# Graph attention on one core: products of a quarter and their sums in separate steps

## The chip, the cores and the metric

The kernel runs on one core of a Trainium2 chip. The core has five engines that are used here: TensorE (PE; its weight loads are listed as PEld), VectorE (DVE), ScalarE (ACT), GpSimd (POOL) and SyncE (SP), each with its own queue of instructions in a fixed order. An instruction waits at the head of its queue until what it needs is there, and everything behind it waits too. The metric is the device time of one execution in microseconds (us); shown is the median of three.

## The reference

A small graph network on 12500 nodes of 128 features and 200000 edges: a two-layer graph convolution with a layer norm, then an attention over the edges, with a second layer norm. The part that matters here is the attention, with `row` the source and `col` the destination of an edge:

```python
scores = einsum('ehd,ehd->eh', q[row], k[col]) / sqrt(16) + edge_emb @ eb_w.T + eb_b
seg_max = segment_max(scores, row)
exp_scores = exp(scores - seg_max[row])
attn = exp_scores / (segment_sum(exp_scores, row)[row] + 1e-10)
out = segment_sum(attn[..., None] * v[col], row)
```

There are 8 heads of 16 features.

## The kernel before

The kernel sorts the edges first, then does the two rounds of the convolution (spread and sum), the node layers between them, and then the attention; a last node stage writes the output. The change touches the attention alone, the function `attention`.

The edges are sorted by source node and cut into tiles of 128 edges, so that all edges of a tile belong to one block of 128 nodes. Four tiles (`G`) are a quarter, four quarters (`QN`) a group of 2048 edges; there are 104 groups, 416 quarters, 1664 tiles. The loop at the end of `attention` runs over steps `s`, one new quarter a step; in a step each stage works on an older quarter, and how much older is set by the constants `EXPAND, SCORE, WEIGH, ADD`.

- `take` (step s): POOL gathers the k and v rows of four tiles from DRAM into `kvg`, by indirect DMA, with 11 buffers (`KVB`), one for each quarter in flight.
- `turn` (every second step): VectorE builds `oht`, the one-hot matrices that pick an edge's source node, for two quarters.
- `expand` (quarter s - 2): TensorE makes q[row] of four tiles, `qe`, by `oht` times the block of `q_all`; the number of the block is fetched into a register of TensorE's queue first (line 889).
- `score` (quarter s - 3): VectorE multiplies `qe` with the gathered k and sums over each head into `sc`.
- `maxima`: once per group, a chain in seven pieces over TensorE, VectorE and ScalarE that finds the running maximum of each node. `sc` is completed (L1281) and turned (`st`, L1283), scanned both ways (`fw`, `bw`), the ends turned (`ro`, L1291 and L1292), copied by ScalarE (L1295, L1296), scanned along the tiles (`lu`, L1303 and L1305), turned back (`near`, `cp`, `cs`), combined (`mxs`, `dt`), turned (`wt`, `mr`, L1329 and L1331); ScalarE writes the exponentials into `kvg`, and a last pair (`dl`, L1339) gives the factor `fall` by which older sums shrink. The loop lets the chain go on by one piece at each `yield` of the other two generators. So its first piece comes at the end of the step in which the group's last quarter was scored, and all others in the next step, here called the chain step.
- `mark` (quarter s - 9): ScalarE builds `oh`, the one-hot matrix for the sum.
- `weigh` (quarter s - 9): VectorE multiplies v by the exponentials (L1358).
- `add_up` (quarter s - 10): for each of four tiles TensorE makes the product `ps` of `oh` and the weighted rows (L1379, 136 columns: 128 sums and 8 denominators), and VectorE adds it to the node block in `acc1` (L1381, the last of a quarter L1384), whose block number it fetches into a register. `ps` has three PSUM buffers of one bank each; the addition of a tile is issued after the product and the fetch of the next one. With a group's first quarter, the old sums are first scaled by `rs` (L1371, L1373, L1376).

PSUM has eight banks: two for `qe`, three for the buffers with the tag "g", which the chain's tiles `st`, `ro`, `cp`, `wt`, `mr` and also `rs` share, and three for `ps`.

The order of instructions in each queue is the order in which the program issues them; no planner moves them. In a step TensorE's queue holds `qe` of one quarter and `ps` of another, with pieces of the chain between and before them. VectorE's holds weigh, multiply, reduce, then the additions, with pieces of the chain between them. (`weigh` is called before the generators run.)

Of the kernel before, what the change touches and what calls it, by code (L numbers as in the profile page):

```python
# [9 lines left out]
F32 = mybir.dt.float32  # L10
# [6 lines left out]
P = 128  # L17
H = 8
HD = 16
W = P + H  # L20
G = 4
# [58 lines left out]
def kernel(  # L80
# [21 lines left out]
    nc = tc.nc  # L102
# [41 lines left out]
    ident = const.tile([P, P], F32, name="ident")  # L144
# [1056 lines left out]
    def attention(wp, psp):  # L1201
# [4 lines left out]
        T = TPP  # L1206
        QN = T // G
        kvs, scs, ohts, seqs, recs, mks, gts, ohs, fall = ({} for _ in range(9))
        a17 = wp.tile([1, H, T + 1], F32, name="a17")
# [66 lines left out]
        def maxima(g):  # L1276
# [4 lines left out]
            nc.vector.tensor_add(sc, sc, recs.pop(g)[:, :, :H].rearrange("p t h -> p h t"))  # L1281
            st = psp.tile([P, P], F32, tag="g", name="st", bufs=3)
            nc.tensor.transpose(st, sc.rearrange("p h t -> p (h t)"), ident)  # L1283
# [5 lines left out]
                                         op0=ALU.add, op1=ALU.max)  # L1289
            ro = psp.tile([1, 2, P], F32, tag="g", name="ro", bufs=3)  # L1290
            nc.tensor.transpose(ro[:, 0, :], fw[:, P - 1:], ident)  # L1291
# [20 lines left out]
            for k in range(2):  # L1312
                nc.vector.tensor_tensor(
                    near[:, k], luv[:, k, :, k:k + T],
                    gc[:, k * T:(k + 1) * T].unsqueeze(1).to_broadcast([1, H, T]), op=ALU.add)
            cp = psp.tile([P, 2], F32, tag="g", name="cp", bufs=3)
            for k in range(2):
# [9 lines left out]
            nc.vector.tensor_tensor(dt, st, mxs, op=ALU.subtract)  # L1327
            wt = psp.tile([P, H, T], F32, tag="g", name="wt", bufs=3)
            nc.tensor.transpose(wt.rearrange("p h t -> p (h t)"), dt, ident)  # L1329
            mr = psp.tile([1, H, T], F32, tag="g", name="mr", bufs=3)  # L1330
            nc.tensor.transpose(mr.rearrange(flat), mxs[:, :1], ident)  # L1331
            for q in range(QN):
# [22 lines left out]
        def weigh(i):  # L1355
# [3 lines left out]
                                 .to_broadcast([P, G, H, HD]))  # L1359

        def add_up(i):

            g, q = divmod(i, QN)
            t = kvs.pop(i)
            o = ohs.pop(i)
            for k in range(G):
                b = block_no(blk_si, i * G + k, [DVE])
                a = acc1[:, ds(b, 1), :].rearrange("p o w -> p (o w)")
                if q == 0 and k == 0:
                    rs = psp.tile([P, H], F32, tag="g", name="rs", bufs=3)  # L1370
                    nc.tensor.matmul(rs, o[0:1, 0, :], fall.pop(g), start=True, stop=True)  # L1371
                    av = a[:, :P].rearrange("p (h d) -> p h d", h=H)
                    nc.vector.scalar_tensor_tensor(  # L1373
                        av, rs.unsqueeze(2).to_broadcast([P, H, HD]), 1.0, av,
                        op0=ALU.add, op1=ALU.mult)
                    nc.vector.scalar_tensor_tensor(a[:, P:], rs, 1.0, a[:, P:],  # L1376
                                                   op0=ALU.add, op1=ALU.mult)
                ps = psp.tile([P, W], F32, name="ps", bufs=3)
                nc.tensor.matmul(ps, o[:, k, :], t[:, k, P:], start=True, stop=True)  # L1379
                if k:  # L1380
                    nc.vector.tensor_add(*adds)  # L1381
                    yield
                adds = a, a, ps
            nc.vector.tensor_add(*adds)  # L1384
            yield


        EXPAND, SCORE, WEIGH, ADD = 2, 3, 9, 10
        NQ = NG * QN
# [4 lines left out]
        for s in range(NQ + ADD):  # L1394
# [12 lines left out]
            if 0 <= s - EXPAND < NQ:  # L1407
                expand(s - EXPAND)
            i = s - SCORE
            bulk = []  # L1410
# [107 lines left out]
```

## Time and profile before

| what | value |
|---|---|
| median of three runs | 10037.43 us (10016.77 to 10048.95) |
| the profiled execution's own time | 8137.72 us |
| its span, first to last instruction | 8135.9 us |
| attention, first gather to last addition | about 5527 to 7980 us |
| busy in the span: PE, DVE, POOL, ACT | 71%, 70%, 55%, 26% |
| mean granted TensorE clock | 0.813 (about 0.72 in the attention) |
| a group of the attention, mean over 103 | 23.35 us |

The profile is of one execution, and that one was some 1900 us shorter than the median of the plain runs. Durations below are from it. A timeline row gives start, duration, engine, line, operation, output and inputs, and in brackets the idle time of the engine before it with what ended it. "Issue" is idle time in which the engine waited for nothing that the profile shows, such as a register fetch. The granted clock of TensorE is 1 at full and 0.5 at half speed; matrix instructions of f32 come in pairs (two passes), so four `ps` products are 8 instructions.

### The profile page before, as it was taken

What the parts mean: (1) busy time and instruction counts of PE and PEld (TensorE: products, weight loads), DVE (VectorE), ACT (ScalarE), POOL (GpSimd) and SP (SyncE); (2) the same over time, 40 slices, a digit from 0 to 9 for tenths busy, and PEclk for the clock granted to TensorE, in tenths of its full rate; (3) what the DMA queues carried; (4) which work ended last, traced back from release to release, by engine and by line L of the source; (5) the groups of instructions that cost most, each with busy time, mean ns of one, the idle gap of its engine ahead of it and who ended that gap; (6) DMA issues with size and microseconds to landing.
All of it is one profiled execution on the core that took longest, in us unless ns stands there. A gap on an engine that the chain in (4) does not pass through costs nothing.

```text
span 8135.9 us, 117573 instructions
## 1 busy us (share of the span) xinstructions
PE 5811.8 (71%) x32059; PEld 4415.2 (54%) x32059; DVE 5697.5 (70%) x11412; ACT 2087.4 (26%) x5494; POOL 4507.0 (55%) x4450
## 2 busy tenths in 40 slices
PE   5777781222899988859993788536777777777775
PEld 2344440121677777747772777535655566666564
DVE  8988785986555688765552666676777777777778
ACT  1222220001344300014441000013444444444442
POOL 0000005872777677777777777506666666666660
PEclk9999895555999999979996999867777777777775
DMA  3333233001577677736663666634444444444463
GB/s 84 94 90 94 84 106 90 6 5 29 157 197 197 198 209 204 195 48 194 196 195 78 193 192 193 147 114 140 123 123 124 120 124 123 124 119 123 124 114 71
DMA packets 570541, 1045.40 MB, mean 128 GB/s; under 512 B 131594, under 2 KB 294678, under 8 KB 557252
## 3 DMA queue, kind: packets, MB, share of 16 engines
q0 software_dynamic: 220992, 514.28, 26.6%
q1 hardware_dynamic: 348928, 523.60, 19.7%
q8 instruction: 297, 4.87, 0.2%
q14 instruction: 324, 2.65, 0.1%
HBM read 722.51 MB, written 314.96 MB: 128 GB/s over the span
## 4 chain that ended last, share of the span: by engine, by line
PE 32%; DVE 31%; DMA 12%; issue 10%; POOL 10%; DVEq 3%; ACT 2%; SPq 1%; POOLq 0%; ACTq 0%
PE ex L1016 13%; DMA got<-msg,idx_b 9%; DVE count_oh L234 6%; DVE key_d L460 4%; PE bc L1002 4%; POOL got L809 4%; POOL placed L809 4%; PE qe L1259 3%; DVE acc L1381 3%; POOL kvg L809 2%; DVE key_s L460 2%; PE ps L1379 2%; DVE kvg L1358 2%; PE bp L764 2%; DVE kvg L1269 2%
## 5 line engine op out<-in xcount | busy, mean ns | idle before, releaser
L809 POOL DMA_INDIRECT kvg<-kv,rec_in x1664 | 1634.1, 982 | 1073.1 <-issue 430.1
L809 POOL DMA_INDIRECT placed<-rec,idx_s x1664 | 1729.1, 1039 | 588.1 <-issue 503.0
L1055 PE MATMUL ps<-got,oh 128*128 128x128 f32 x8704 | 1214.0, 290 | 420.4 <-DMA got<-msg,idx_b 238.5
L1055 PEld LDWEIGHTS ps<-got,oh 128*128 128x128 f32 x8704 | 1073.2, 196 | 561.1 <-DVE acc L1061 261.6
L809 POOL DMA_INDIRECT got<-msg,idx_b x1088 | 1116.9, 1027 | 382.4 <-issue 130.7
L1007 DVE TENSOR_SCALAR oht<-bc,iota_col 128x512 f32<-128x512 f32 x976 | 732.3, 751 | 696.4 <-PE bc L1002 695.8
L1016 PE MATMUL ex<-h_all,oht 128*128 x7808 | 1134.7, 289 | 0.0
L1016 PEld LDWEIGHTS ex<-h_all,oht 128*128 128x128 f32 x7808 | 949.1, 192 | 222.3 <-issue 220.5
L1379 PE MATMUL ps<-kvg,oh 128*128 128x136 f32 x3328 | 785.8, 378 | 241.4 <-DVE acc L1381 240.8
L1259 PE MATMUL qe<-q_all,oht 128*128 x3328 | 902.7, 409 | 53.0 <-DVE oht L1248 11.2
L1259 PEld LDWEIGHTS qe<-q_all,oht 128*128 128x128 f32 x3328 | 685.9, 257 | 270.1 <-issue 189.2
L1379 PEld LDWEIGHTS ps<-kvg,oh 128*128 128x128 f32 x3328 | 635.6, 263 | 324.3 <-DVE acc L1381 308.7
L1020 ACT COPY et<-ex 128x512 f32<-128x512 f32 x976 | 571.3, 585 | 819.2 <-PE ex L1016 367.4
L1047 DVE TENSOR_TENSOR oh<-loc_b,iota_row 128x512 f32<-128x512 f32 x1088 | 753.8, 693 | 18.8
L1381 DVE TENSOR_TENSOR acc<-acc,ps 128x136 f32 x1248 | 365.7, 293 | 445.8 <-PE ps L1379 234.7
L949 POOL IOTA iota_t<- 128x1664 f32 x1 | 1.5, 1528 | 1165.2 <-PE pair_ps L239 1165.2
L1061 DVE TENSOR_TENSOR acc<-acc,ps 128x128 f32 x1088 | 308.7, 284 | 411.3 <-PE ps L1055 407.8
L1351 ACT ACTIVATE sq<-iota_row,loc_s 128x128 f32<-128x128 f32 x1664 | 529.8, 388 | 10.1
L751 ACT COPY attr_t<-tp 128x512 f32<-128x512 f32 x391 | 228.7, 585 | 955.8 <-PE tp L749 955.8
L764 PE MATMUL bp<-attr_t,ebw_at 128*64 128x512 f32 x782 | 444.2, 651 | 1.6 <-DVE attr_t L753 1.6
L1002 PE MATMUL bc<-seq_l,ones_bf 1*128 1x512 bf16 x976 | 377.1, 387 | 56.8 <-DMA seq_l<-seq_a 56.8
L460 DVE TENSOR_TENSOR key_s<-key_s 128x512 f32<-128x512 f32 (+1 forms) x468 | 397.6, 903 | 25.9 <-ACT key_s L475 23.1
(361 smaller groups left out, 6818.3 us busy)
## 6 DMA issues: line engine op xcount, KB each, us to landing
msg<-et SPq DMA_DIRECT2D x488, 258.0 KB
msg<-et SPq DMA_DIRECT2D x488, 256.0 KB
attr<-in_edge_attr_dram SPq DMA_DIRECT2D x97, 896.0 KB
seq_in<-row_seq SPq DMA_DIRECT2D x104, 512.0 KB
placed<-rec,idx_s POOLq DMA_INDIRECT x1664
kvg<-kv,rec_in POOLq DMA_INDIRECT x1664
got<-msg,idx_b POOLq DMA_INDIRECT x1088
masks<-mk SPq DMA_DIRECT2D x16, 832.0 KB
```

Source lines behind the costliest of these rows:

```text
L460: nc.vector.tensor_tensor(to, lo, hi, op=op)
L764: nc.tensor.matmul(sums[i // RQ][:RQ * H].rearrange("h g p -> h (g p)"), ebw_at[:, (RQ - 1 - r) * H:(2 * RQ - 1 - r) * H], tts.pop(i).rear ...
L809: nc.gpsimd.indirect_dma_start(out=out_, out_offset=None, in_=table, in_offset=bass.IndirectOffsetOnAxis(ap=idx, axis=0))
L1002: nc.tensor.matmul(bcs[t], ones_bf[:1, :], seqs[t // SQ][:, t % SQ * SA:][:, :SA], start=True, stop=True)
L1007: nc.vector.tensor_scalar(ohs[t].rearrange("p k c -> p (k c)"), bcs.pop(t), iota_col, None, op0=ALU.is_equal)
L1016: nc.tensor.matmul(exs[t][:, k, :], o[:, k, :], hb, start=True, stop=True)
L1020: nc.scalar.copy(ets[t][:, :, :D], exs.pop(t))
L1047: nc.vector.tensor_tensor(oh[t], loc_b[:, t, :].unsqueeze(2).to_broadcast([P, R, P]), iota_row.unsqueeze(1).to_broadcast([P, R, P]), op=AL ...
L1055: nc.tensor.matmul(ps[t], o[:, k, :], x_[:, k, :D], start=(k == 0), stop=(k == R - 1))
L1259: nc.tensor.matmul(qe[:, k, :], o[:, c * P:(c + 1) * P], qb, start=True, stop=True)
L1379: nc.tensor.matmul(ps, o[:, k, :], t[:, k, P:], start=True, stop=True)
L1381: nc.vector.tensor_add(*adds)
```

## The change

- `add_up` is split. A new `total` issues all four products of a quarter on TensorE, into two PSUM tiles of two products each (280 columns: two of 136 and 8 for `rs`). `add_up` does only the additions, a step later, each right after the fetch of its block number.
- `ps` has four buffers of one bank. The chain's `st` and `wt` share one bank (`sw`), and `ro`, `cp` and `mr` another (`sm`), with a single buffer each; `rs` lies in the first tile of `ps`.
- The constants go from `EXPAND, SCORE, WEIGH, ADD = 2, 3, 9, 10` to `EXPAND, SCORE, WEIGH, TOTAL, ADD = 1, 2, 8, 9, 10`: everything between the gather and the products comes one step earlier, the additions stay where they were. The gather's 11 buffers are freed by `total`.
- In the loop `total` is called after `expand`, before the generators. So in TensorE's queue the four products follow `qe` at once, and all pieces of the chain that belong to the step come after them: `ro` before stood ahead of the products and now stands behind them, and `cp` before stood ahead of the fourth product.
- With the lags, a group's chain step is now at step 4g + 6 (before 4g + 7). `turn` runs at even steps, before at a step ahead of and after the chain step, now in it; the scaling with `rs` before came in the step ahead of the chain step and is now in it.

```diff
--- before.py
+++ after.py
@@ -1205,7 +1205,7 @@
 
         T = TPP
         QN = T // G
-        kvs, scs, ohts, seqs, recs, mks, gts, ohs, fall = ({} for _ in range(9))
+        kvs, scs, ohts, seqs, recs, mks, gts, ohs, fall, sums = ({} for _ in range(10))
         a17 = wp.tile([1, H, T + 1], F32, name="a17")
         f17 = wp.tile([1, H, T + 1], F32, name="f17")
         loc_s = wp.tile([P, NT], F32, name="loc_s")
@@ -1279,7 +1279,8 @@
             mk = mks.pop(g)
             gl, gc = gts.pop(g)
             nc.vector.tensor_add(sc, sc, recs.pop(g)[:, :, :H].rearrange("p t h -> p h t"))
-            st = psp.tile([P, P], F32, tag="g", name="st", bufs=3)
+            sw = psp.tile([P, 2, P], F32, name="sw", bufs=1)
+            st, wt = sw[:, 0, :], sw[:, 1, :].rearrange("p (h t) -> p h t", h=H)
             nc.tensor.transpose(st, sc.rearrange("p h t -> p (h t)"), ident)
             yield
             fw = wp.tile([P, P], F32, name="fw", bufs=1)
@@ -1287,7 +1288,9 @@
             bw = wp.tile([P, P], F32, name="bw", bufs=1)
             nc.vector.tensor_tensor_scan(bw[:, ::-1], mk[:, 1, ::-1], st[:, ::-1], NEG,
                                          op0=ALU.add, op1=ALU.max)
-            ro = psp.tile([1, 2, P], F32, tag="g", name="ro", bufs=3)
+            sm = psp.tile([P, 4 * P], F32, name="sm", bufs=1)
+            ro = sm[:1, :2 * P].rearrange("o (k c) -> o k c", k=2)
+            mr, cp = sm[:1, 2 * P:3 * P], sm[:, 3 * P:3 * P + 2]
             nc.tensor.transpose(ro[:, 0, :], fw[:, P - 1:], ident)
             nc.tensor.transpose(ro[:, 1, :], bw[:, :1], ident)
             was = wp.tile([1, H], F32, name="was", bufs=2)
@@ -1313,7 +1316,6 @@
                 nc.vector.tensor_tensor(
                     near[:, k], luv[:, k, :, k:k + T],
                     gc[:, k * T:(k + 1) * T].unsqueeze(1).to_broadcast([1, H, T]), op=ALU.add)
-            cp = psp.tile([P, 2], F32, tag="g", name="cp", bufs=3)
             for k in range(2):
                 nc.tensor.matmul(cp[:, k:k + 1], near[:, k].rearrange(flat), one,
                                  start=True, stop=True)
@@ -1325,10 +1327,9 @@
                                                op0=ALU.add, op1=ALU.max)
             dt = wp.tile([P, P], F32, name="dt", bufs=1)
             nc.vector.tensor_tensor(dt, st, mxs, op=ALU.subtract)
-            wt = psp.tile([P, H, T], F32, tag="g", name="wt", bufs=3)
             nc.tensor.transpose(wt.rearrange("p h t -> p (h t)"), dt, ident)
-            mr = psp.tile([1, H, T], F32, tag="g", name="mr", bufs=3)
-            nc.tensor.transpose(mr.rearrange(flat), mxs[:, :1], ident)
+            nc.tensor.transpose(mr, mxs[:, :1], ident)
+            mr = mr.rearrange("o (h t) -> o h t", h=H)
             for q in range(QN):
                 nc.scalar.activation(
                     kvs[g * QN + q][:, :, 2 * P:],
@@ -1358,34 +1359,40 @@
             nc.vector.tensor_mul(v, v, kvs[i][:, :, 2 * P:].unsqueeze(3)
                                  .to_broadcast([P, G, H, HD]))
 
+        def total(i):
+
+            g, q = divmod(i, QN)
+            t, o = kvs.pop(i), ohs.pop(i)
+            two = []
+            for k in range(G):
+                if k % 2 == 0:
+                    two.append(psp.tile([P, 2 * W + H], F32, name="ps", bufs=4))
+                if q == 0 and k == 0:
+                    nc.tensor.matmul(two[0][:, 2 * W:], o[0:1, 0, :], fall.pop(g),
+                                     start=True, stop=True)
+                nc.tensor.matmul(two[-1][:, k % 2 * W:][:, :W], o[:, k, :], t[:, k, P:],
+                                 start=True, stop=True)
+            sums[i] = two
+
         def add_up(i):
 
-            g, q = divmod(i, QN)
-            t = kvs.pop(i)
-            o = ohs.pop(i)
+            two = sums.pop(i)
             for k in range(G):
                 b = block_no(blk_si, i * G + k, [DVE])
                 a = acc1[:, ds(b, 1), :].rearrange("p o w -> p (o w)")
-                if q == 0 and k == 0:
-                    rs = psp.tile([P, H], F32, tag="g", name="rs", bufs=3)
-                    nc.tensor.matmul(rs, o[0:1, 0, :], fall.pop(g), start=True, stop=True)
+                if i % QN == 0 and k == 0:
+                    rs = two[0][:, 2 * W:]
                     av = a[:, :P].rearrange("p (h d) -> p h d", h=H)
                     nc.vector.scalar_tensor_tensor(
                         av, rs.unsqueeze(2).to_broadcast([P, H, HD]), 1.0, av,
                         op0=ALU.add, op1=ALU.mult)
                     nc.vector.scalar_tensor_tensor(a[:, P:], rs, 1.0, a[:, P:],
                                                    op0=ALU.add, op1=ALU.mult)
-                ps = psp.tile([P, W], F32, name="ps", bufs=3)
-                nc.tensor.matmul(ps, o[:, k, :], t[:, k, P:], start=True, stop=True)
-                if k:
-                    nc.vector.tensor_add(*adds)
-                    yield
-                adds = a, a, ps
-            nc.vector.tensor_add(*adds)
-            yield
-
-
-        EXPAND, SCORE, WEIGH, ADD = 2, 3, 9, 10
+                nc.vector.tensor_add(a, a, two[k // 2][:, k % 2 * W:][:, :W])
+                yield
+
+
+        EXPAND, SCORE, WEIGH, TOTAL, ADD = 1, 2, 8, 9, 10
         NQ = NG * QN
         for g in range(3):
             load_records(g)
@@ -1406,6 +1413,8 @@
                 turn(s // 2)
             if 0 <= s - EXPAND < NQ:
                 expand(s - EXPAND)
+            if 0 <= s - TOTAL < NQ:
+                total(s - TOTAL)
             i = s - SCORE
             bulk = []
             if 0 <= i < NQ:
```

## The prediction

> **What bounds the kernel now.** I read the page's slices first: the attention stage is the last 30% of the span (about 5527 to 7980 us), where PE, DVE and POOL all stand near 7 tenths and none is full. So the limit is an order, not a load. Next came the stage's waits, then the timeline of one group of four quarters. A group is delimited by its one `sc` addition (L1281); 104 of them from 5551.1 to 7956.1 us make 23.35 us a group on average. The group below, 6578.15 to 6601.46, has 23.31. First its three stretches, in the table of busy time by window (length, busy us of each engine, granted TensorE clock):
>
> ```profile
> core 0: us, PE busy (x) PEld busy (x) DVE busy (x) ACT busy (x) POOL busy (x), PEclk, DMA share, GB/s
> 6578.15:6582.59 4.44, 3.97 (x16) 3.45 (x17) 3.23 (x10) 0.41 (x2) 3.25 (x4) 0.53 0.67 212
> 6582.59:6586.93 4.34, 3.07 (x11) 1.94 (x10) 2.83 (x12) 0.58 (x4) 1.59 (x2) 0.50 0.27 79
> 6586.93:6601.46 14.53, 11.03 (x50) 8.96 (x50) 11.18 (x27) 8.84 (x26) 10.69 (x11) 0.82 0.37 108
> ```
>
> The stretches are `sc` to `lu` (L1303), `lu` to `dl` (L1339), and `dl` to the next `sc`. Over all groups their means are 4.51, 4.17 and 14.67 us (medians 4.46, 4.34, 14.53). DVE is busy 17.2 us of 23.3; TensorE runs at half clock in the first two. VectorE's timeline of the round before (start, duration, idle time before it and who ended it):
>
> ```profile
> 6568.72 0.68 DVE L1358 TENSOR_TENSOR kvg<-kvg 128x512 f32<-128x512 f32 x1
> ...
> 6570.03 0.69 DVE L1271 TENSOR_REDUCE sc<-kvg 128x32 f32<-128x512 f32 x1
> 6570.97 0.30 DVE L1381 TENSOR_TENSOR acc<-acc,ps 128x136 f32 x1 [0.24 <-issue]
> 6571.58 0.29 DVE L1381 TENSOR_TENSOR acc<-acc,ps 128x136 f32 x1 [0.32 <-DVE acc L1381]
> ...
> 6572.60 0.30 DVE L1384 TENSOR_TENSOR acc<-acc,ps 128x136 f32 x1
> 6572.81 0.75 DVE L1248 TENSOR_SCALAR oht<-seq_in,iota_col 128x1024 f32<-128x1024 bf16 x1
> ...
> 6575.40 0.28 DVE L1373 SCALAR_TENSOR_TENSOR acc<-rs,acc 128x128 f32 x1
> 6575.71 0.17 DVE L1376 SCALAR_TENSOR_TENSOR acc<-rs,acc 128x8 f32 x1
> 6576.31 0.30 DVE L1381 TENSOR_TENSOR acc<-acc,ps 128x136 f32 x1 [0.43 <-DVE acc L1376]
> ...
> 6578.15 0.38 DVE L1281 TENSOR_TENSOR sc<-sc,rec_in 128x128 f32<-128x128 f32 x1
> ...
> 6582.37 0.29 DVE L1381 TENSOR_TENSOR acc<-acc,ps 128x136 f32 x1 [1.21 <-PE ps L1379]
> 6582.59 0.42 DVE L1303 TENSOR_TENSOR_SCAN lu<-gl_in,a 1x136 f32<-1x136 f32 x1
> ...
> 6586.93 0.15 DVE L1339 TENSOR_TENSOR dl<-was,mr 1x8 f32<-1x8 f32 x1 [0.64 <-PE mr L1331]
> ```
>
> An ordinary step lasts 4.09 us (6568.72 to 6572.81). Additions follow at 0.62 us though each takes 0.30: the block number is fetched into a register before each (0.30 us for the fetch, 0.09 for the address, on VectorE's own queue), and whether the products are there hardly matters. Only in the chain step does VectorE really wait for TensorE: 1.21 us before 6582.37. TensorE's timeline shows why:
>
> ```profile
> 6576.66 0.50 PE L1379 MATMUL ps<-kvg,oh 128*128 128x136 f32 x2 [1.57 <-DVE acc L1381]
> 6578.59 0.47 PE L1283 MATMUL st<-ident,sc 128*128 128x128 f32 x1 [1.43 <-DVE sc L1281]
> 6579.09 2.36 PE L1259 MATMUL qe<-q_all,oht 128*128 x8
> 6581.25 0.42 PE L1291 MATMUL ro<-ident,fw 128*1 128x128 f32 x1
> ...
> 6581.68 1.57 PE L1379 MATMUL ps<-kvg,oh 128*128 128x136 f32 x6
> ```
>
> TensorE idles 1.57 and 1.43 us, then takes `st`, a whole quarter of `qe`, and only then `ro`, which the chain needs. So `sc`, `st`, `qe`, `ro`, two ScalarE copies, `lu` is the path. The gathers are no bound: POOL needs some 1.25 us for each of 16, so 20 us of 23.3, and what it waits for is a buffer that the products free:
>
> ```profile
> POOL kvg L809 <- PE ps L1379: 314.6, 194, 3.5
> ```
>
> **The change, part by part.** No work goes away: per group the same 32 `qe` and 32 `ps` instructions on TensorE, the same 16 additions and 16 register fetches on VectorE, the same gathers and the same SyncE queue. Everything lies in order and waits.
>
> *Sums a step after their products; fetch, then add.* Before, two fetches stood ahead of a quarter's first addition and none ahead of its last: gaps 0.24, 0.32, 0.32, 0.10. After, each addition has one. The first is covered by the reduction (0.69 us over 0.39 us); the spacing is 0.62 throughout. Step: weigh to multiply 0.60, to reduce 0.71, to the first addition 0.61, three times 0.615, 0.21 to the end: 3.98 instead of 4.09. Where a fetch turned out uncovered, the step would stay at 4.10.
>
> *Lags of one step less.* `oht` (L1248) comes every second step and the `rs` scaling (L1373, L1376) in every fourth; before, both `oht` lie in the stretch `dl` to `sc`, and `rs` too. After, the chain runs at step 4g+6: one `oht` (0.66 us) and `rs` fall into the chain step, ahead of `lu`, where VectorE has nothing better to do. New stretch `dl` to `sc`: 0.33 (the two `dl`) + 0.66 + 3 x 3.98 = 12.93, against 0.33 + 2 x 0.66 + 2 x 4.09 + 4.69 (the step with `rs`) = 14.52. Against the mean, 14.67, it saves 1.74 us; the 0.15 are scattered waits for `ps` that go away.
>
> *Products of a quarter as one lump.* TensorE's queue for the chain step is now `st`, four `qe`, all four `ps` (8 instructions), then `ro`, `cp`, `wt`, `mr`. Before, `ro` came ahead of `ps`. The 8 cost 1.87 us at half clock (six in 1.57, the last alone 0.41, so 0.234 each) or 1.15 at full (six in 0.86 earlier in the same trace). `ro` moves from 3.10 us after `sc` (3.18 in the mean) to 4.97. From `ro` to `lu` it took 1.34, because `lu` stands behind an addition that waited for `ps`; free of that, the ScalarE copy of `ro` ends 0.92 after `ro` starts, so 0.97. `sc` to `lu`: 4.51 + 1.87 - 0.37 = 6.01. Is VectorE there by then? 0.35 + `oht` 0.66 + weigh 0.60 + multiply 0.61 + two scans 0.64 + reduce 0.58 + `mxs` 0.45 (with the fetch) + `rs` 0.62 + addition 0.22 = 4.73. So it waits 1.3 us for `ro`: the wait before the addition becomes one before `lu`, and the moved `oht` and `rs` do lie in its cover.
>
> *Which clock in the chain step?* At half clock `sc` to `lu` is 6.01. At full clock `ro` stands at 0.43 + 0.33 + 1.98 + 1.15 = 3.9, `lu` could go at 4.8, and VectorE's own 4.73 decides. The Trainium skill ("TensorE: Matmul & The Clock Gate", Part 1) says that the clock falls to half after at least one idle window of about 3.4 us and returns after one busy window. After the change TensorE finishes the last round's products early and stands idle some 3 us (by my layout from about 10.2 to 13.4 us after `dl`) before `st`; by the rule this is not a full window and the chain could run at full clock. The row says otherwise: 1.57 + 1.43 us idle, split, was enough, since `st` is at its slow duration in most groups and `ro` in all (0.42):
>
> ```profile
> L1283 PE MATMUL st<-ident,sc x104: 330/474/477, 5551.5 to 7956.6; 128*128 128x128 f32 x104
> ```
>
> I follow the row: half clock. By the rule the group would be 12.93 + 4.75 + 3.74 (`lu` to `dl` where `cp` is fast, the least in the trace) = 21.4, a saving of 1.9 us.
>
> *PSUM banks, single `sw` and `sm`.* Four `ps` banks hold two quarters, so TensorE may run a quarter ahead; their reuse waits for additions a full step earlier, and at half clock TensorE needs 3 x (2.16 + 1.87) + 0.45 = 12.5 us for what lies between `mr` and `st`, under the 13.4 there is. `st`, `wt` and `ro`, `cp`, `mr` share banks but follow one another by data anyway: nothing, and at most the 0.2 us or so of a semaphore if they don't. `lu` to `dl` stays 4.17; the fetch now ahead of the fourth addition hides in the 0.64 us wait for `mr`. Gathers get their buffer at the same distance (four steps) from its use as before: nothing, with 3 us of POOL idle a group as cover.
>
> *Sum.* 12.93 + 6.01 + 4.17 = 23.11 against 23.35: 0.24 us a group, times 104 = 25 us. The profiled execution took 8137.72 us (span 8135.9), so 8113, or -0.31%. The median of the plain runs is 10037, 1900 us more, and nothing in the profile tells where those lie; I carry the ratio over: 10037 x 0.9969 = 10006. If the extra time is elsewhere, the 25 us stay 25 and it is 10012.
>
> **Rivals.** (1) *The chain runs at full clock:* 1.9 x 104 = 200 us, 2.5% of 8138, so 9790. For it: VectorE then is the only bound and TensorE has denser lumps. Against it: the slow `st` and `ro` rows. A clock that rises midway gives parts of it (0.72 us of the products: 75 us, 9945).
> (2) *Slower: the lump ahead of `ro` costs more than the stretch gives back.* The price is 1.50 us at `sc` to `lu`; it decides as soon as `dl` to `sc` shrinks by less. If only the moved `oht` and `rs` (0.66 + 0.60 = 1.26) go and the fetch gaps stay, and `cp` stays slow in every group (4.34 for 4.17), that is +0.41 us a group, 43 us, 10090. For it: every addition now has its fetch directly ahead. Against it: the first addition's gap is marked "issue", two fetches long.
> (3) *Nothing:* in plain runs, 1900 us longer, gathers may be what paces the stage (at over 1.45 us each they would, 16 x 1.45 = 23.3), or the gain stays under what can be told: 10037, 10010 to 10065. Against it: in the trace POOL waits for the products.
>
> **How the numbers follow.** Forecast as laid out 0.42 (its own range 9970 to 10030), full or partly full clock 0.18, slower 0.25, nothing 0.15. About 0.3% (30 us) is what a measurement of this kernel tells from no change. Of the forecast's 0.42, some 0.27 is beyond it, 0.12 within, 0.03 above; so faster 0.27 + 0.18 = 0.45, same 0.12 + 0.15 = 0.27, slower 0.25 + 0.03 = 0.28. The predicted time is 10006. The range reaches to the partly full clock and some way past it, and to the slower case: 9860 to 10095.
>
> **What would show it.** Right: `dl` to `sc` near 12.9 us, ordinary steps of 3.98, hardly any VectorE wait for `ps`, `ro` some 5 us after `sc`, a new VectorE wait of about 1.3 us before `lu`, ended by ScalarE's copy, half clock there. Wrong: `st` and `ro` at 0.33 and below 0.4 (rival 1); steps still at 4.1 (rival 2); POOL without waits (rival 3); or `st` starting well over 0.43 us after `sc`, which would mean that TensorE came late.

## The result, and the profile after

The changed kernel takes 9884.0 us (median of 4 plain runs, 9871.7 to 9916.8); the kernel before took 10032.9 on the same chip (10016.8 to 10049.0). The ratio is 0.9857, with a 95% interval of 0.9826 to 0.9888: 149 us faster, where 25 to 31 were forecast. The sign and the range held; the size did not, and most of what follows is about the other 120 us.

The profile that the prediction worked from was of an execution 1900 us shorter than any plain run of the same kernel; the kernel before was therefore profiled once more, and that second profile (span 10032.3 us) and the one of the changed kernel (span 9894.2 us) both agree with the plain runs, so they are what is compared here.

The whole difference lies in the attention stage. The stage begins at nearly the same time in both (first `sc` at 7100 and 7109 us), and what follows the last `sc` takes 180 us before and 181 after. From one `sc` to the next a group takes 26.72 us before and 25.29 after: 1.43 us, which over the 103 intervals from the first `sc` to the last is 147. By stretches, means over all groups:

| stretch | profile of the prediction | second profile of before | changed kernel | predicted change | measured change (last two profiles) |
|---|---|---|---|---|---|
| `sc` to `lu` | 4.51 | 4.81 | 8.52 | +1.50 | +3.71 |
| `lu` to `dl` | 4.17 | 4.15 | 4.36 | 0 | +0.21 |
| `dl` to the next `sc` | 14.67 | 17.77 | 12.37 | -1.74 | -5.40 |

One group of each follows, as busy time by window (length, busy us of each engine, TensorE clock). The kernel before, second profile:

```profile
core 0: us, PE busy (x) PEld busy (x) DVE busy (x) ACT busy (x) POOL busy (x), PEclk, DMA share, GB/s
8368.68:8373.18 4.50, 4.05 (x16) 3.44 (x17) 3.20 (x9) 0.41 (x2) 3.38 (x4) 0.50 0.60 192
8373.18:8376.92 3.74, 2.10 (x11) 1.30 (x10) 2.89 (x11) 0.47 (x3) 0.94 (x1) 0.86 0.20 69
8376.92:8394.79 17.87, 11.76 (x50) 9.07 (x50) 11.31 (x27) 8.84 (x27) 11.29 (x12) 0.71 0.32 95
```

The changed kernel, the same three stretches:

```profile
8121.39:8130.96 9.57, 4.58 (x19) 3.83 (x19) 4.32 (x13) 0.29 (x2) 5.58 (x7) 0.76 0.50 158
8130.96:8135.34 4.38, 1.70 (x7) 1.33 (x8) 2.97 (x10) 0.70 (x5) 3.46 (x4) 0.50 0.30 78
8135.34:8147.56 12.22, 9.39 (x50) 8.32 (x50) 9.88 (x25) 8.83 (x26) 6.27 (x8) 0.78 0.28 80
```

VectorE is busy 17.4 us of 26.1 and 17.2 of 26.2 in these two groups: what changes is where it waits. Its groups by line, between 7200 and 9700 us (count | busy us, mean ns | idle us before, and who ended it), first the kernel before in the second profile, 94 groups:

```profile
L1381 DVE TENSOR_TENSOR acc<-acc,ps 128x136 f32 x1131 | 331.6, 293 | 578.4 <-remote 173.6 <-PE ps L1379 170.7 <-DVE acc L1381 73.3
...
L1384 DVE TENSOR_TENSOR acc<-acc,ps 128x136 f32 x377 | 110.5, 293 | 34.5 <-issue 3.2 <-remote 1.1 <-PE qe L1259 1.0
...
L1373 DVE SCALAR_TENSOR_TENSOR acc<-rs,acc 128x128 f32 x94 | 27.3, 291 | 125.5 <-remote 86.9 <-PE ps L1379 32.7 <-issue 5.1
```

then the changed kernel, 100 groups:

```profile
L1391 DVE TENSOR_TENSOR acc<-acc,ps 128x136 f32 x1589 | 465.4, 293 | 257.7 <-issue 130.3 <-DVE acc L1391 119.0 <-remote 3.4
...
L1306 DVE TENSOR_TENSOR_SCAN lu<-gl_in,a 1x136 f32<-1x136 f32 x100 | 42.7, 427 | 210.7 <-ACT a L1298 204.3 <-issue 6.3
L1287 DVE TENSOR_TENSOR_SCAN fw<-mk_in,sw 128x128 f32<-128x128 bf16 x100 | 41.8, 418 | 172.9 <-PE ps L1373 150.8 <-PE qe L1259 9.0 <-remote 7.7
```

Before, the additions and the `rs` scaling wait (578.4 + 34.5 + 125.5) / 94 = 7.9 us a group. After, the additions wait 2.6 us, for register fetches ("issue" and one another) and hardly any longer for TensorE. In exchange `lu` waits 2.1 and `fw` 1.7. "Remote" here means that the releasing matmul had ended long before by its record. (Where the row of `fw` names `ps`, that is only the matmul recorded last before the release; what `fw` reads is `st`, which stands ahead of it in TensorE's queue.) These waits are the part which the first profile did not have. The end of the `dl`-to-`sc` stretch in the kernel before shows them, VectorE's timeline first (start, duration, idle before):

```profile
8389.96 0.29 DVE L1373 SCALAR_TENSOR_TENSOR acc<-rs,acc 128x128 f32 x1 [0.81 <-PE ps L1379]
...
8392.82 0.29 DVE L1381 TENSOR_TENSOR acc<-acc,ps 128x136 f32 x1 [2.37 <-remote]
8393.58 0.29 DVE L1381 TENSOR_TENSOR acc<-acc,ps 128x136 f32 x1 [0.47 <-remote]
```

and TensorE's:

```profile
8387.77 1.67 PE L1379 MATMUL ps<-kvg,oh 128*128 128x136 f32 x6
8393.17 0.82 PE L1379 MATMUL ps<-kvg,oh 128*128 128x136 f32 x2 [3.73 <-DVE acc L1381]
```

By the records the first three products were done at 8389.4; the additions that take them could start at 8392.8 and later. I call such a completion *late*. The ends of TensorE's records are modelled, so "late" is measured against the record; the waits of VectorE are measured. In the changed kernel the additions hardly feel it, but the chain does. VectorE's timeline of the chain step of the group above:

```profile
8119.55 0.29 DVE L1391 TENSOR_TENSOR acc<-acc,ps 128x136 f32 x1
8120.03 0.30 DVE L1391 TENSOR_TENSOR acc<-acc,ps 128x136 f32 x1 [0.20 <-issue]
8120.64 0.30 DVE L1391 TENSOR_TENSOR acc<-acc,ps 128x136 f32 x1 [0.31 <-issue]
8121.18 0.29 DVE L1391 TENSOR_TENSOR acc<-acc,ps 128x136 f32 x1 [0.24 <-DVE acc L1391]
8121.39 0.38 DVE L1281 TENSOR_TENSOR sc<-sc,rec_in 128x128 f32<-128x128 f32 x1
...
8125.48 0.29 DVE L1391 TENSOR_TENSOR acc<-acc,ps 128x136 f32 x1
8130.96 0.43 DVE L1306 TENSOR_TENSOR_SCAN lu<-gl_in,a 1x136 f32<-1x136 f32 x1 [5.18 <-ACT a L1298]
```

TensorE's and ScalarE's in the same step:

```profile
8121.83 0.33 PE L1284 MATMUL sw<-ident,sc 128*128 128x128 f32 x1 [3.33 <-DVE acc L1391]
8122.33 0.48 PE L1259 MATMUL qe<-q_all,oht 128*128 x2 [0.17 <-PE sw L1284]
8123.02 1.85 PE L1259 MATMUL qe<-q_all,oht 128*128 x6 [0.21 <-issue]
8124.67 1.90 PE L1373 MATMUL ps<-kvg,oh 128*128 128x136 f32 x8
8126.41 0.27 PE L1294 MATMUL sm<-ident,fw 128*1 128x128 f32 x1
```
```profile
8130.67 0.25 ACT L1298 COPY a<-sm 1x128 f32<-1x128 f32 x1 [12.75 <-remote]
```

The order is the predicted one: `st`, four `qe`, eight `ps` instructions, `ro` at 5.0 us after `sc`, TensorE idle 3.3 us before `st`. But ScalarE's copy of `ro` starts 4 us after `ro` ended by its record. It does so in 45 of the 104 groups; their median period is 26.8 us, that of the others 23.7. In 53 of the other 59, `st` is the late one and `fw` waits for it for over 1 us.

### The profile page after: what moved, and what is told of

It is laid out like the page before. It is cut to its first block, busy times and chain, and to the rows that moved or that the text cites. A ratio compares the mean times of both kernels' runs of the same rounds, so it can differ in the third digit from the quotient of the medians.

```text
span 9894.2 us, 116212 instructions
## 1 busy us (share of the span) xinstructions
PE 5956.3 (60%) x32059; PEld 4658.6 (47%) x32059; DVE 5676.0 (57%) x11412; ACT 2079.2 (21%) x5494; POOL 4477.8 (45%) x4450
## 4 chain that ended last, share of the span: by engine, by line
PE 27%; another core or an unknown queue 15%; DVE 11%; issue 9%; ACT 3%; DVEq 2%; DMA 1%; POOL 1%; ACTq 0%; POOLq 0%; SPq 0%
PE ps L1055 13%; PE ex L1016 7%; PE qe L1259 2%; PE bc L1002 2%; PE ps L1373 2%; DVE acc L1391 1%; ACT sq L1352 1%; DVE kvg L1359 1%; DVE kvg L1269 1%; DVEq L889 1%; ACT oh L1354 1%; DMA got<-msg,idx_b 1%; PE n_mp L864 1%; DVE acc L1061 1%
## 5 line engine op out<-in xcount | busy, mean ns | idle before, releaser
L1016 PE MATMUL ex<-h_all,oht 128*128 x7808 | 1380.1, 331 | 815.3 <-DVE oht L1007 516.0
L1016 PEld LDWEIGHTS ex<-h_all,oht 128*128 128x128 f32 x7808 | 1174.0, 231 | 1090.2 <-issue 578.7
L1055 PE MATMUL ps<-got,oh 128*128 128x128 f32 x8704 | 1242.8, 302 | 576.3 <-DVE acc L1061 287.6
L1055 PEld LDWEIGHTS ps<-got,oh 128*128 128x128 f32 x8704 | 1140.4, 210 | 678.6 <-DVE acc L1061 338.9
L1259 PE MATMUL qe<-q_all,oht 128*128 x3328 | 842.5, 403 | 75.1 <-DVE kvg L1269 29.6
L1391 DVE TENSOR_TENSOR acc<-acc,ps 128x136 f32 x1664 | 487.5, 293 | 271.4 <-issue 135.2
L1373 PE MATMUL ps<-kvg,oh 128*128 128x136 f32 x3328 | 639.2, 352 | 1.4 <-DVE acc L1391 0.7
L1373 PEld LDWEIGHTS ps<-kvg,oh 128*128 128x128 f32 x3328 | 593.2, 259 | 6.1 <-DVE acc L1391 1.8
L1002 PE MATMUL bc<-seq_l,ones_bf 1*128 1x512 bf16 x976 | 425.0, 436 | 0.0
L460 DVE TENSOR_TENSOR key_d<-key_d 128x512 f32<-128x512 f32 (+1 forms) x468 | 397.9, 904 | 37.3 <-ACT key_d L475 18.6
```

Of the source, the lines that this page charges most:

```text
L1002: nc.tensor.matmul(bcs[t], ones_bf[:1, :], seqs[t // SQ][:, t % SQ * SA:][:, :SA], start=True, stop=True)
L1016: nc.tensor.matmul(exs[t][:, k, :], o[:, k, :], hb, start=True, stop=True)
L1055: nc.tensor.matmul(ps[t], o[:, k, :], x_[:, k, :D], start=(k == 0), stop=(k == R - 1))
L1259: nc.tensor.matmul(qe[:, k, :], o[:, c * P:(c + 1) * P], qb, start=True, stop=True)
L1373: nc.tensor.matmul(two[-1][:, k % 2 * W:][:, :W], o[:, k, :], t[:, k, P:], start=True, stop=True)
L1391: nc.vector.tensor_add(a, a, two[k // 2][:, k % 2 * W:][:, :W])
```

## The experiments

Theory A is the prediction's own sum: the order alone makes the gain. Theory B: the gain is that additions a step behind their products no longer feel TensorE's late completions. The runs after the first four ask where the lateness comes from, T (TensorE has too much work; some expectations call it L) against I (it is late after idling), and whether it can be hidden. Ratios are to the kernel before, timed beside each kernel; beside the last two it ran at 9926 and 9915 us, so ratios are compared, not times.

VectorE's idle time by what it stands before, us per group (sums over groups 4 to 101 of each profile; additions include the `rs` scaling):

| kernel | ratio (95%) | group | additions | `fw` | `lu` | `mxs`, `dl` | multiply (`qe`) | all but additions |
|---|---|---|---|---|---|---|---|---|
| before, first profile | | 23.3 | 4.68 | 0 | 0 | 1.16 | 0 | 1.16 |
| before, second profile | 0.9996 (0.9984-1.0008) | 26.5 | 7.87 | 0 | 0 | 1.10 | 0 | 1.10 |
| the change | 0.9857 (0.9826-0.9888) | 25.1 | 2.64 | 1.72 | 2.07 | 1.12 | 0.07 | 4.98 |
| lags_only | 0.9931 (0.9912-0.9949) | 25.8 | 7.14 | 0 | 0 | 1.12 | 0 | 1.12 |
| split_only | 0.9840 (0.9824-0.9857) | 24.9 | 2.64 | 1.35 | 2.41 | 0.94 | 0.06 | 4.76 |
| ro_first | 0.9886 (0.9869-0.9902) | 25.4 | 2.64 | 1.16 | 2.99 | 1.13 | 0.03 | 5.30 |
| fill8 | 0.9750 (0.9729-0.9770) | 24.2 | 2.63 | 2.83 | 0.14 | 1.13 | 0.03 | 4.12 |
| fill8_mid | 0.9796 (0.9776-0.9816) | 24.6 | 2.73 | 0.12 | 1.40 | 1.21 | 1.59 | 4.31 |
| qe_ahead | 0.9758 (0.9738-0.9777) | 24.3 | 2.63 | 2.99 | 0.15 | 1.17 | 0 | 4.31 |
| both_ahead | 0.9803 (0.9772-0.9833) | 24.5 | 2.63 | 3.28 | 0 | 1.22 | 0 | 4.50 |
| light_qe | 0.9855 (0.9838-0.9873) | 25.2 | 2.64 | 0 | 4.01 | 1.12 | 0 | 5.14 |
| late_chain | 0.9755 (0.9739-0.9771) | 24.1 | 2.34 | 0 | 1.68 | 1.55 | 1.11 | 4.34 |
| late_chain2 | 0.9759 (0.9720-0.9797) | 24.0 | 2.09 | 0.01 | 0 | 4.20 | 0.51 | 4.72 |
| late_chain3 | 0.9733 (0.9700-0.9766) | 23.9 | 2.17 | 0 | 0.01 | 3.79 | 0.66 | 4.47 |

**The kernel before again** (no edit).

> The kernel before, unchanged, for a second profile of it: the changed kernel's profiled execution took 9896 us, as its plain runs do, while that of the kernel before took 8138 against plain runs of about 10030. Theory A (the order of the work alone gives the gain): if the profiled time is again near 8138, groups take 23.3 us and nothing is learnt; if it is near 10030, the stages outside the attention are as long as after the change, and the groups are 25.3 + 149/104 = 26.7 us, with the 1.43 us in the stretch from dl to the next sc and few TensorE completions late. Theory B (products a step ahead of their sums hide late TensorE completions): groups of 26.7 us too, but with several us in sum per group of waits of VectorE before additions that end 4 us or more after the matmul's end, which the changed kernel does not have there.

Its profile took 10032 us. Over the groups of the table a group is 3.2 us longer than in the first profile, and the waits of the additions alone are 3.2 us longer (7.87 for 4.68), as theory B says.

**Lags alone.**

```
-        EXPAND, SCORE, WEIGH, ADD = 2, 3, 9, 10
+        EXPAND, SCORE, WEIGH, ADD = 1, 2, 8, 9
```

> Only the lags are changed (1, 2, 8, 9 instead of 2, 3, 9, 10); each addition stays in the step of its product. Theory A: one oht comparison (0.66 us) and the rs scaling (0.60 us) move into the chain step, under a wait of 1.21 us, and ro stays ahead of the products: up to 1.2 us a group, 104 x 1.2 = 125 us, so about 9905 us. Theory B: the additions are as exposed as before, so at most a quarter of the gain: 9995 to 10035 us. Rival C (the moved work delays the scores of the chain step): slower, 10060 us.

9959 us, 0.7% faster: between the two numbers, so neither theory had this one. The gain is about half of what A gave at most to the moved `oht` and `rs`, and the additions still wait 7.1 us.

**The split alone**: the change with the lags of before.

```
-        EXPAND, SCORE, WEIGH, TOTAL, ADD = 1, 2, 8, 9, 10
+        EXPAND, SCORE, WEIGH, TOTAL, ADD = 2, 3, 9, 10, 11
```

> Products and sums in separate steps, with the new PSUM layout, and the lags as before (2, 3, 9, then 10 for the products and 11 for the sums). Theory A: the lump of eight products ahead of ro costs 1.50 us, the fetch gaps and scattered waits give back 4 x 0.11 + 0.15 = 0.6 us: +0.9 us a group, +94 us, so about 10125 us. Theory B: most of the gain is here, 9890 to 9930 us.

9862 us, theory A's sum off by 260 us and on the wrong side; B had the direction, and its range began 28 us higher. The split with its PSUM layout makes the whole gain; the shorter lags on top of it add nothing that can be told (0.9840 against 0.9857, the intervals overlap). Split and PSUM layout were not separated. The split could not have been run in the old layout: with one product to a bank, eight banks would be needed for the products alone. The new layout with each addition still in the step of its product was not run, so the layout's own share is not shown.

**`ro` ahead of the products** in TensorE's queue.

```
-            if 0 <= s - TOTAL < NQ:
-                total(s - TOTAL)
+            due = [s - TOTAL] if 0 <= s - TOTAL < NQ else []
...
                     if chain is not None and not step(chain):
                         chain = None
+                    if due:
+                        total(due.pop())
```

> The changed kernel with the products of the chain step issued after ro instead of ahead of it. Theory A: ro comes 1.87 us earlier, VectorE's own work (4.73 us from sc to lu) then decides instead of 6.0: 1.3 us a group, 135 us less than the changed kernel's 9884, so about 9750 us. Theory B (late TensorE completions set the chain): the copy of ro waits for them whatever stands ahead of it, so 9840 to 9884 us. Rival C: the products now stand ahead of cp, which waits at half clock: 9884 to 9920 us.

9906 us. `ro` does come earlier, 4.09 us after `sc` for 5.24 in the means, but its copy is late in 67 groups instead of 45, and taking the lump away gains nothing. The time lies in rival C's range and just outside B's, but C's wait is not there: before `mxs`, which takes `cp`, VectorE waits 0.89 us a group for 0.88 in the changed kernel, while before `lu` it waits 2.99 for 2.07.

**More work for TensorE, in two places.** The four products of one quarter are issued twice more into an unread part of the bank, once per group: in the step that ends with the idle stretch, or in the step before that one. (The cut leaves out that the tile of the bank is widened to hold them.)

```
+            for k in range(8 if q == 0 else 0):
+                nc.tensor.matmul(two[1][:, 2 * W:][:, :W], o[:, k % G, :], t[:, k % G, P:],
+                                 start=True, stop=True)
```

(the second kernel has `q == 3`)

> The changed kernel with work added: eight more products of the quarter that is summed first in each group (one in four), written to an unread part of its PSUM bank, so that TensorE has work in the 3 us that it idles ahead of st. Nothing of the result changes. Theory I (TensorE is slow to complete after an idle stretch; its ro is 4 to 5 us late in some 45 of 104 groups for that): the late copies of ro go (218 us) and st, qe and ps run at full clock: 9884 - 220 - 80 = 9580 us. Theory L (completions come late because TensorE has done too much in the time before): the added work makes more of them late: 9900 to 9990 us. Neither (the added work is hidden and changes nothing): 9884 us.

> The same eight products added to the last quarter of the group instead, two steps ahead of st, where TensorE is busy already. Theory I: the idle stretch ahead of st is as long as before, so nothing is gained: 9884 us, or the 1 to 2 us that the products take where VectorE waits for them, up to 9990. Theory L: as many late completions as with the products in the other place: the same time as there.

9785 and 9842 us; no theory had either number. Useless work makes the kernel faster in both places, which speaks against L; but theory I is not right either. In the first place late `ro` fall from 45 groups to 2, and `st` stands at full clock in 103 of 104, yet `fw` now waits for `st`. VectorE's groups of that kernel, 7200 to 9400 us, 91 groups:

```profile
L1306 DVE TENSOR_TENSOR_SCAN lu<-gl_in,a 1x136 f32<-1x136 f32 x91 | 38.4, 422 | 13.8 <-ACT a L1298 13.6
L1287 DVE TENSOR_TENSOR_SCAN fw<-mk_in,sw 128x128 f32<-128x128 bf16 x91 | 38.3, 421 | 256.5 <-PE ps L1373 203.0 <-remote 53.5
```

So of the change's 4.98 us of waits outside the additions only 0.86 went; the rest moved.

**The real work ahead of `st`**: the chain step's `qe`, or its `qe` and `ps`, issued at the end of the step before.

```
+                if s + 1 - EXPAND < NQ:
+                    expand(s + 1 - EXPAND)
+                if s + 1 - TOTAL >= 0:
+                    total(s + 1 - TOTAL)
                 chain = maxima(i // QN)
                 step(chain)
```

(the first kernel without the two lines of `total`; in the next step they are skipped)

> The changed kernel with the four qe of the chain step issued ahead of st instead of behind it: real work in the idle stretch, and none is added. By the sum of the prediction ro comes 1.98 us earlier and VectorE's own 4.73 us decides: 1.28 us a group, 133 us, 9750 us. Theory I: the idle stretch shrinks from 3.1 to about 1.2 us, half of the late copies go as well: 9640 us. Theory L: late completions stay, 9750 us at best.

> The changed kernel with the four qe and the four products of the chain step issued ahead of st. The last products wait for the additions that free their bank, so st comes up to 0.9 us later, and ro follows st at once: sc to ro about 2.2 us, VectorE's own 4.73 us decides: 9750 us by the sum. Theory I: hardly any idle time, no late copies of ro: 9600 us. Theory L: 9750 us or more, the late completions move to the products and to st.

9795 and 9834 us: the first better than the change by some 1.0%, the second by 0.5%, where the intervals touch. The sums of the prediction and theory I gave more than was found. L set only a lower bound, 9750 us, and that held in both, as did its forecast that the late completions move to `st`: the waits end where the first of the filled kernels had them, before `fw` (2.99 and 3.28 us). That L is wrong all the same is for the next run to show.

**Less work for TensorE.** Three of four `qe` are made from bf16 constants, so three quarters of the scores are wrong; TensorE has 63 matrix records a group for 75.

```
+                if k == 0:
                     nc.tensor.matmul(qe[:, k, :], o[:, c * P:(c + 1) * P], qb, ...)
+                else:
+                    nc.tensor.matmul(qe[:, k, :], ones_bf, iota_bf, start=True, stop=True)
```

> The changed kernel with three of the four qe products of a quarter replaced by products of two bf16 constants (so three quarters of the scores are wrong); all waits, fetches and VectorE work are as before. It takes some 5 us of matrix work a group from TensorE. Theory T (in plain runs TensorE is behind its records because it has too much work, and VectorE waits for it): fw and lu no longer wait (3.8 of 25.1 us a group), so up to 390 us: 9500 to 9650 us. Theory I (TensorE is slow to complete after low activity, which more work cured): as many late completions or more, lower clock: 9850 to 9980 us.

9872 us: no faster than the change, and in the range of theory I. `fw` never waits, `lu` waits 4.0 us, and the copy of `ro` is late in 97 of 104 groups. VectorE's two lines, 7200 to 9600 us, 96 and 95 groups:

```profile
L1310 DVE TENSOR_TENSOR_SCAN lu<-gl_in,a 1x136 f32<-1x136 f32 x96 | 41.2, 429 | 389.2 <-ACT a L1302 387.0 <-issue 2.1
L1291 DVE TENSOR_TENSOR_SCAN fw<-mk_in,sw 128x128 f32<-128x128 bf16 x95 | 39.0, 410 | 0.5 <-PE ps L1377 0.5
```

Theory T falls: TensorE is not late because it has too much to do. The number, the lower clock (0.726 for 0.749) and the many late copies are what theory I forecast; but by that theory the filled kernels should have lost their waits, and they only moved them.

**The chain spread over two, then three steps**, so that VectorE has other work between a request to TensorE and the use of the answer. The edits, not shown, are bare `yield`s between the chain's pieces in `maxima` (and 6 for 4 in the pacing of the steps); the kernels over three steps have WEIGH, TOTAL, ADD at 9, 10, 11.

> The changed kernel with the chain spread over two steps: fw and bw behind the first addition of the chain step, lu behind the multiply of the step after it, near behind its reduction, dt behind its second addition, dl behind its last; VectorE's other work stands between each request to TensorE and the use of its answer. The waits of VectorE for TensorE before fw, lu, mxs and dl (1.72 + 2.07 + 0.88 + 0.24 = 4.9 of 25.1 us a group) get covers of 1.2 to 3.4 us. If TensorE only answers late (theory I or the order): 3.5 to 4.9 us a group, 360 to 510 us less: 9370 to 9520 us, and the gathers (20 us a group) begin to pace. If TensorE has too much work (theory T): the waits reappear before other instructions, 9750 us or more.

> The chain spread over three steps (lu behind the first addition of the step after the chain step, near behind its second; dt behind the multiply of the third step, dl behind its first addition), with lags 1, 2, 9, 10, 11 so that the exponentials are there in time. Between ro and lu, and between near and mxs, VectorE now has about a step of other work, 4 to 5 us, more than a late completion has taken there. If a late completion of TensorE can be covered: lu 1.68 and mxs 1.52 of 24.1 us a group go, 330 us less than with the chain over two steps (9779): about 9450 us, with gathers near 20 us a group next. If TensorE is late by a fixed amount once a group wherever VectorE asks for its work, the waits reappear before the multiply that takes qe, the additions or fw: 9740 to 9800 us.

> As the chain over three steps, with dl three more pieces later, at the end of the third step: the wait before dl (3.96 of 24.0 us a group in the kernel before this one) gets some 2 us more of other VectorE work ahead of it. If each late answer can be covered once VectorE asks late enough: 2 us a group, 0.979 of that kernel's time, a ratio to the kernel before of about 0.955. If TensorE is late by a fixed amount once a group, the wait moves on to another instruction and the ratio stays at 0.974 to 0.978.

Ratios 0.9755, 0.9759 and 0.9733. The first, 9779 us, is again a number that T forecast (9750 or more, with the waits back before other instructions). The run with less work speaks against T; what holds of its forecast here is that the waits move. Over two steps the wait before `fw` goes and those before `mxs` and the multiply grow; over three steps those before `lu` and `mxs` go as well and 4 us stand before `dl`. VectorE's `lu` and `dl` over three steps (the kernel before the last, 7200 to 9400 us):

```profile
L1312 DVE TENSOR_TENSOR_SCAN lu<-gl_in,a 1x136 f32<-1x136 f32 x92 | 39.1, 425 | 0.3
...
L1349 DVE TENSOR_TENSOR dl<-was,sm 1x8 f32<-1x8 f32 x91 | 13.6, 149 | 359.2 <-remote 342.1 <-PE qe L1259 17.2
```

With `dl` moved back by some 2 us more (the last run) it still waits 338.5 us in 93 groups. Covering the wait did not shorten it: in all eleven kernels that have the split, VectorE waits 4.1 to 5.3 us a group outside the additions, wherever the requests stand. The last one, at 0.9733, has the lowest ratio and beats the change by 1.3%; it cannot be told from `late_chain`, `late_chain2`, `fill8` and `qe_ahead`, whose intervals overlap with its own.

## Why the prediction was right or wrong

- **The sign was right, but not for its reason.** `dl` to `sc` was to shrink and `sc` to `lu` to grow, with a small net gain. Both held, and `ro` came at 5.24 us (5.17 in the median) for 4.97. But most of the gain was to come from the moved `oht` and `rs`; by the same sum the split without the shorter lags makes the kernel slower, 10125 us. It ran at 9862 and has the whole gain.
- **The range held by luck.** Its lower part, down to 9860, was there for a TensorE at full or partly full clock. 9884 was reached by another way, waits that the additions no longer feel.
- **The failed step is the term of `dl` to `sc`:** "whether the products are there hardly matters", and the wait for `ps` that goes away put at 0.15 us. In the first profile that is what stood there. In the profile that agrees with the plain runs the additions wait 7.87 us a group instead of 4.68, so the term was short by 3.2 us. The prediction saw the 1900 us of difference, wrote that nothing tells where they lie, and carried the ratio over, as though they lay evenly. They lie for the most part in waits for TensorE: some 1550 us ahead of the attention stage (the last section has them), and 330 us among the very additions that the change frees.
- **Spacing of the additions.** Predicted 0.615 throughout; the timeline above shows 0.61 only where the addition opens a bank (0.31 us before it), and 0.48 and 0.54 for the others. That is 0.2 us a step, and three steps of it make up the difference between the 12.37 us of the stretch and the 12.93 forecast.
- **`sc` to `lu`, +1.50 predicted, +3.71 measured.** The new wait before `lu`, ended by ScalarE's copy, was put at 1.3 us and is 2.1; a wait before `fw` (1.7 us) was not forecast at all. Both are late completions. What the lump itself costs is not shown: without it (ro_first) the kernel is no faster, and more copies of `ro` are late. Rival 2 falls with the measured time; the additions of a step stand closer than forecast, not wider.
- **The clock.** The prediction followed the row, half clock in the chain step. The measured clock is mixed. `st` is at its half-clock duration in 65 of 104 groups, where it was so in all 104 of the second profile of before; `ro`, at 421 ns in nearly all groups before, is anywhere between (minimum, median, maximum 270, 372, 421 ns). The rows of `st` (minimum, median, maximum in ns), second profile of before and then the changed kernel:

```profile
L1283 PE MATMUL st<-ident,sc x104: 446/475/478, 7100.4 to 9852.9; 128*128 128x128 f32 x104
```
```profile
L1284 PE MATMUL sw<-ident,sc x104: 328/473/477, 7109.0 to 9714.1; 128*128 128x128 f32 x104
```

  The Trainium skill ("TensorE: Matmul & The Clock Gate", Part 1) has the clock fall only after a whole idle window of about 3.4 us. TensorE mostly idles 3.0 to 3.5 us before `st`, and 57 of the 65 slow `st` follow a gap below 3.4 us, so the rule alone does not give them. Neither does it in the run with less work, where `st` is slow in 101 groups after a median gap of 2.9 us. Where added products filled the gap, to 1.3 us, `st` ran at full clock in 103 groups. Rival 1 did not follow: a faster clock does not bring the answers earlier when they are late.
- **`lu` to `dl`, predicted unchanged:** +0.21. The wait before `mxs`, for `cs`, grows by 0.3 us and the one before `dl` shrinks by as much; the fetches of the additions in this stretch were not hidden, as the prediction had them, and cost 0.16.
- **Rival 3, gathers pace the plain runs:** their own time does not. GpSimd still waits for the products to free a buffer, less than before (635.6 us in the second profile of before):

```profile
POOL kvg L809 <- PE ps L1373: 280.6, 120, 9.0
```

The corrected sum, per group of the table: waits of the additions 7.87 to 2.64, waits outside them 1.10 to 4.98, VectorE's busy time 0.09 less: -5.23 + 3.88 - 0.09 = -1.44 us, where these groups measure -1.39 and all groups -1.43.

## What to carry to other kernels

Compare the profiled execution with the plain runs before anything is summed from it: when they differ by a fifth, take another profile, because the missing time can sit in particular waits, as here, and not in proportion. Putting a consumer one step behind its producer is worth more than the producer's duration suggests when completions come late; but look for the next instruction that asks the same engine, since that is where the lateness turns up. A wait that only moves when it is given cover, as here in kernel after kernel, suggests a cause outside the order of the work.

## What the hardware showed that was not expected

TensorE's completions reach VectorE and ScalarE late, and almost only while GpSimd issues its indirect DMAs. I counted every wait of VectorE and ScalarE for TensorE over 0.6 us ahead of the attention stage, by whether an indirect DMA ran on GpSimd between 1.5 us before and 0.3 us after the recorded end of the last matmul before the release. In the second profile of the kernel before, 368 of the 946 waits with one were over 1 us late, and 2 of the 1320 without. What the waits beside GpSimd took over 0.3 us sums to 1780 us; these stages take 7100 us there and 5551 in the first profile, which has 1705 waits beside GpSimd and not one of them late. The twelve other profiles repeat the second: 351 to 397 late of about 900 to 950 with an indirect DMA, 0 to 7 of about 1300 without. In the attention stage of the second profile it is 147 of 626 with a gather and 1 of 114 without. It is not a matter of which matmul is waited for: of VectorE's waits for `bc` (L1002), one and the same instruction, 134 of 260 were late beside an indirect DMA and 1 of 535 without. In the other direction nothing is late: in some 600 waits of TensorE for VectorE and 140 for ScalarE the release came within 0.02 us of the other's recorded end.

Traffic of the DMA engines as such is not enough. Around 1092 of the 1320 waits without an indirect DMA the 16 DMA engines were busy for a fifth of the time or more (mean over the engines, 1.5 us on either side of the matmul's end), and none of these waits was late.

The lateness is plain in the spread stage of the second profile: VectorE first, then GpSimd, whose batch of 16 begins and ends here, then two of TensorE's `bc`:

```profile
2246.16 0.75 DVE L1007 TENSOR_SCALAR oht<-bc,iota_col 128x512 f32<-128x512 f32 x1 [0.66 <-issue]
2248.16 0.75 DVE L1007 TENSOR_SCALAR oht<-bc,iota_col 128x512 f32<-128x512 f32 x1 [1.25 <-PE bc L1002]
2255.25 0.75 DVE L1007 TENSOR_SCALAR oht<-bc,iota_col 128x512 f32<-128x512 f32 x1 [6.34 <-remote]
2266.57 2.07 DVE L1007 TENSOR_SCALAR oht<-bc,iota_col 128x512 f32<-128x512 f32 x3 [10.57 <-remote]
2270.09 0.75 DVE L1007 TENSOR_SCALAR oht<-bc,iota_col 128x512 f32<-128x512 f32 x1 [1.45 <-PE bc L1002]
```
```profile
2243.82 0.94 POOL L809 DMA_INDIRECT placed<-rec,idx_s  x1 [14.88 <-DMA rec_s<-placed]
...
2262.56 0.94 POOL L809 DMA_INDIRECT placed<-rec,idx_s  x1 [0.30 <-issue]
```
```profile
2248.55 0.38 PE L1002 MATMUL bc<-seq_l,ones_bf 1*128 1x512 bf16 x1
...
2251.36 0.39 PE L1002 MATMUL bc<-seq_l,ones_bf 1*128 1x512 bf16 x1
```

By the order of both queues, the third VectorE line takes the first of these `bc`, which had ended at 2248.9 by its record; even the second had ended at 2251.7. Three microseconds after GpSimd's last instruction everything is on time again. The longest delays are in the stage between the two layers: of twelve matmuls recorded within 2.9 us, VectorE took the first eight 20 us after their recorded end, ScalarE the last four 30 us after theirs.

This is a correlation in the traces, not an experiment: no run here changed the gathers, and none tells their issue on GpSimd from the transfers that they start. It fits that in the attention stage, where GpSimd issues 16 gathers a group, no order of TensorE's and VectorE's work got rid of the 4 to 5 us. Why one execution of the same program had none of it stays open, and so does the mechanism. It is also not shown why, in the attention stage, the lateness falls on `ro` in one group and on `st` in the next.
